# Issuing TensorE, VectorE and ScalarE in program order through the woven stretches of a four-layer network

## The chip, the cores and the metric

The kernel runs on one core of one Trainium2 chip, in fp32 throughout. The metric is the device time of one execution in microseconds (us), as the median of several runs; lower is better. One further execution is recorded by the hardware profiler. Its span, from the first instruction to the last, is given beside its own time.

## The reference

The input `x` is 8 images of 56 x 56 positions with 192 channels. Each of four layers adds something to it. Each layer first normalises it with a group norm `_gn` over 32 groups (a sample's groups of 6 channels over all positions).

```python
# layers 0 and 1
p, q, v = silu(x @ p_w.T + p_b), silu(x @ q_w.T + q_b), silu(x @ v_w.T + v_b)   # 192 -> 576
qv = q * v
o1 = _toeplitz(qv along w, a1)     # a1, a2: from a small MLP of the distance, times a decay
o2 = _toeplitz(qv along h, a2)     # one 56-tap kernel to each side, per channel
x = x + (p * (o1 + o2)) @ o_w.T + o_b          # with x normalised by _gn on the right
# layer 2
y = conv 7x7, depthwise (_gn(x)); y = layernorm(y); x = x + gamma * (gelu(y @ w0 + b0) @ w1 + b1)
# layer 3: attention in shifted 7x7 windows, 6 heads of 32, with position bias and masks
x = x + softmax(q @ k.T * s + bias) @ v @ Wfc + bfc
```

## The kernel before, in words

**Storage.** The 8 samples lie as 4 pairs. A pair's 2 x 192 channels fill three blocks of 128 partitions (128, 128, and 64 + 64). Two pairs are worked on at a time, named by `j0` = 0 or 2. So `Q(1, 2)` is the q and v projection of layer 1 for pairs 2 and 3. Intermediate results (`qv`, `L_sum`, `x1`, `x2`, `yd`) go through DRAM.

**Generators.** Each job is a Python generator that emits a piece of work and then yields the time that its author reckons for it.

- `tno_qv` (L207, called Q): for each of 25 groups of tokens, tile x is normalised on ScalarE (L228). Then come units of 512 output columns (a last one of 128): matmuls on TensorE (L245) into one or two PSUM tiles, a VectorE add of the bias (L254), and, in `multiply`, a Silu on ScalarE (L264), q times v on VectorE (L267) and the store through SP (L270). `multiply` of a unit is emitted at the head of the next unit, ahead of that unit's matmuls.
- `tno_toeplitz` (L317 to L376, called TZ): 18 rounds, an `along` and a `turned` kind in turn for nine blocks of 64 channels and two directions. `along` is TensorE matmuls of a qv tile `q` with Toeplitz matrices `tm` (L343) and a ScalarE copy (L350), in 8 groups. `turned` is 8 groups of TensorE transposes (L360) and a VectorE copy or add (L363, L366). After the eighth group of `along` ScalarE issues the loads for two rounds on: the half L317 (SP issues the other half) or the whole of L320, and two DMAs of L331. Each yield stands for four groups, 3.2 us.
- `tno_out` (called O): 28 steps of 224 tokens. A step has p's projection of this tile and the output projection of the one before, interleaved on TensorE (L460 to L499), Silus on ScalarE (L504, L521), the gate p * (o1 + o2) on VectorE (L531, L532), the residual sums (L514, L517), a POOL store (L115), and the normalisation of the next tile on VectorE (L442), which comes last.
- `conv` (loads L692 and L696): `turn` normalises a tile on ScalarE (L710), transposes it on TensorE (L722), and copies it on VectorE (L733) and ScalarE (L731); there are 7 tiles with two channel blocks (part 0) and 7 with one (part 1). `group` does 7 x 7 taps as 16 matmuls (L742) and a ScalarE copy (L749).
- `mlp`: layer norm (L832 to L844), transposes and scaling (L864, L866), expansion and gelu (L881, L890), and contraction (L961 to L979).
- `attention`: projections (L1102, L1112, L1155), scores (L1185), turned probabilities (L1223 to L1233), weighted sums (L1245), and `out` in two halves (L1271, with VectorE's L1282). The table `order` says at each of four places of a group whether a step of the next unit's projection (0) or of the last unit's `out` (1) is emitted.

**Order of the work.** `weave` runs a lane: it emits a step of the lane's generator, then as many steps of a second generator as its share of the time asks for. Near the end of a job it starts the next one (`begin`), so that its first loads are emitted early; a step that yields None adds no time. The lanes are, in order: Q(0,0); Q(0,2) with TZ(0,0); O(0,0) then Q(1,0) with TZ(0,2); O(0,2) then Q(1,2) with TZ(1,0); O(1,0) with TZ(1,2); O(1,2) with the first convolution; the MLP with the second convolution; the rest of the MLP with the head of the attention; and the attention.

What an engine executes, and in which order, isn't the order of emission: the framework's scheduler chooses for every engine from what has been emitted, by its own estimates. `manual_schedule(engines=...)` switches this off for the named engines within a block; these then get their instructions in the order of the program. The PSUM pool has 4 tiles of two banks (`bank2`); the SBUF pool `tp` has 3 buffers a name (`t6`, `t8`, `t4`), `q` has 2 and `cv`'s x tile 2.

Of the kernel before, what the change touches and what calls it, by code (L numbers as in the profile page):

```python
# [15 lines left out]
AX = mybir.AxisListType  # L16
PSUM = bass.MemoryType.PSUM
DRAM = bass.MemoryType.DRAM

B, H, W, C = 8, 56, 56, 192  # L20
T = H * W
# [10 lines left out]
def view(ap, offset, dims):  # L32

    return bass.AP(ap.tensor, ap.offset + offset, [ap.ap[0], *dims])


class Net:
# [371 lines left out]
        for f in late:  # L409
            store(*f)  # L410

    def tno_out(self, L, j0, xs, gn, o, ys, gn_next):

# [1 line left out]
        N = 224  # L417
# [10 lines left out]
        def load_x(j, t):  # L428

            x = p.tile([128, 3, 2 * N], F32, name="t6")  # L430
            self.load_pair(x, xs, j, slice(t * N, (t + 2) * N))
            return x

        def load_s(j, t):
            s = p.tile([128, 9, N], F32, name="t8")
            nc.sync.dma_start(s, o[j, :, :, t * N : (t + 1) * N].rearrange("k p t -> p k t"))
            return s

        def normalize(j, x):
            xn = p.tile([128, 3, N], F32, name="t4")  # L440
            for k in range(3):
                nc.vector.tensor_scalar(  # L442
                    xn[:, k, :], x[:, k, :], gn[:, j, k, 0:1], gn[:, j, k, 1:2], ALU.mult, ALU.add
                )
            return xn
# [96 lines left out]
        before = None  # L542
        x2 = load_x(*tiles[0])
        s = load_s(*tiles[0])
        yield 0.0
        xn = normalize(j0, x2[:, :, :N])
        done = None
        for n, (j, t) in enumerate(tiles):
            self.norm_part()
# [6 lines left out]
            x = x2[:, :, t % 2 * N : t % 2 * N + N]  # L556
            now = (j, t, x, s, st, xn)
            after = None
            if n + 1 < len(tiles):
# [3 lines left out]
                if t % 2:  # L563
                    x2 = x2_next
                at = (t + 1) % 2 * N
                after = tiles[n + 1][0], x2[:, :, at : at + N]
            xn = step(now, before, after)
# [47 lines left out]
    def tno_layers(self, x0, x1, x2, gn, last):  # L615


        tc, nc = self.tc, self.nc
        LS = ("L0", "L1")
        tables = [  # L620
            [self.dram.tile([D1, 112], F32, name=f"{L}_tab{d}") for d in range(2)] for L in LS
        ]
        qvs = {

            j0: self.dram.tile([D1 // 32, 64 * W, 128], F32, name=f"qv{j0}") for j0 in (0, 2)
        }
        o = [self.dram.tile([B // 2, 9, 128, T], F32, name=f"{L}_sum") for L in LS]
        x = (x0, x1, x2)
        with ExitStack() as ctx, ExitStack() as wqp:
            self.wqp = wqp.enter_context(tc.tile_pool(name="wqp", bufs=1, side="right"))  # L630
            self.tp = ctx.enter_context(tc.tile_pool(name="tp", bufs=3))
            Q = lambda i, j0: self.tno_qv(LS[i], j0, x[i], gn[i], qvs[j0])
            O = lambda i, j0: self.tno_out(LS[i], j0, x[i], gn[i], o[i], x[i + 1], gn[i + 1])
            TZ = lambda i, j0: self.tno_toeplitz(j0, tables[i], qvs[j0], o[i])
            QT, OT, TZT = 25 * 2.25 * 5.3, 28 * 10.7, 8 + 72 * 3.2

            with tc.tile_pool(name="tab", bufs=2) as tab:
                self.input_stats(x0, gn[0], 0, tab)
                self.decay_tables("L0", tab, tables[0])
                first = Q(0, 0)  # L640
                for n in range(20):
                    next(first)
                self.input_stats(x0, gn[0], 2, tab)
                none = tab.tile([112, 512], F32, name="none", bufs=1)
                nc.gpsimd.memset(none, 0.0)
                for qv in qvs.values():
                    to = qv[:, T:].rearrange("n (p k) e -> p n (k e)", p=112)
                    nc.gpsimd.dma_start(to, view(none, 0, [[0, D1 // 32], [1, 512]]))
                self.decay_tables("L1", tab, tables[1])
                lanes = [[(first, QT)], [(Q(0, 2), QT)], [(O(0, 0), OT), (Q(1, 0), QT)]]  # L650
                lanes += [[(O(0, 2), OT), (Q(1, 2), QT)], [(O(1, 0), OT)], [(O(1, 2), OT)]]
                self.weave(lanes[0], after=lanes[1][0][0])
            with tc.tile_pool(name="tz", bufs=1) as self.tz:
                self.tms = []
                for i in range(2):
                    tm = self.tz.tile([120, 32 * H + 8], F32, name=f"tm{i}")
                    nc.gpsimd.memset(tm, 0.0)
                    self.tms.append(tm)
                for n, tz in enumerate((TZ(0, 0), TZ(0, 2), TZ(1, 0), TZ(1, 2))):
                    self.weave(lanes[n + 1], tz, lanes[n + 2][0][0], TZT)  # L660
                    if n == 2:
                        wqp.close()
            self.weave(lanes[5], **last())

# [317 lines left out]
    def attention(self, L, xs, gn3, gnd, ys, vd):  # L984
# [6 lines left out]
        nc, tc, inp = self.nc, self.tc, self.inp  # L991
# [7 lines left out]
        if True:  # L999
# [72 lines left out]
            def normalize(b, ra, rb):  # L1072

                ja, sa = b % 4, b // 4
                gb = gr[ja // 2][:, ja % 2 + 2 * sa]
                for c, n, c2 in ((3, 53, 0), (0, 3, 53)):
                    nc.vector.tensor_scalar(
                        view(xa, c2, [[W, 28], [1, n]]),
                        view(ra, c, [[W, 28], [1, n]]),
                        gn3[:, ja, sa, 0:1],  # L1080
                        gn3[:, ja, sa, 1:2],
                        ALU.mult,
                        ALU.add,
                    )
                    nc.scalar.activation(
                        view(xb, c2, [[W, 16], [1, n]]),
                        view(rb, c, [[W, 16], [1, n]]),
                        AF.Identity,
                        bias=gb[:, 1:2],
                        scale=gb[:, 0:1],  # L1090
                    )
# [229 lines left out]
            late = None  # L1321


            order = ((0, 0, 0, 0), (0, 1, 1, 0), (0, 0, 0, 0))
            for n in range(len(units) + 1):
                if n < len(units):
                    (b, hh), (v, qf, kf) = units[n], now
# [234 lines left out]
```

## Time and profile before

| | us |
|---|---|
| median of 3 runs | 6437.01 (6429.92 to 6446.78) |
| the profiled execution's own time | 6428.51 |
| its span | 6426.7 |
| mean granted TensorE clock | 0.943 |

The span by stretches, each cut at the place where a lane changes, to about 10 us:

| stretch, us | work | length | TensorE busy | clock |
|---|---|---|---|---|
| 0 to 480 | statistics, tables, Q(0,0) | 480 | 393.5 | 0.97 |
| 480 to 1090 | Q(0,2) + TZ(0,0) | 610 | 535.0 | 0.93 |
| 1090 to 1625 | O(0,0) + TZ(0,2) | 535 | 470.5 | 0.93 |
| 1625 to 2085 | Q(1,0) + TZ(0,2) | 460 | 427.0 | 0.98 |
| 2085 to 2660 | O(0,2) + TZ(1,0) | 575 | 509.1 | 0.91 |
| 2660 to 3130 | Q(1,2) + TZ(1,0) | 470 | 437.0 | 0.97 |
| 3130 to 3830 | O(1,0) + TZ(1,2) | 700 | 598.5 | 0.90 |
| 3830 to 4340 | O(1,2) + convolution | 510 | 478.6 | 0.95 |
| 4340 to 4960 | MLP + convolution | 620 | 591.1 | 0.98 |
| 4960 to 5450 | MLP | 490 | 489.9 | 1.00 |
| 5450 to 6427 | attention | 977 | 853.5 | 0.91 |

TensorE's clock is granted by a throttle; 1.00 is full speed, and 0.93 means that some of the stretch ran at less. A busy TensorE at a lower clock takes longer for the same work, so busy time alone doesn't show it. In the profile, PE is TensorE, DVE VectorE, ACT ScalarE, POOL GpSimd and SP SyncE; a trailing q (ACTq) is the engine's instruction sequencer, which issues its DMAs. "PE bank L360 <- ACT ot L350" reads: TensorE, about to run line 360 for tile `bank`, waited for ScalarE's line 350, which writes `ot`.

### The profile page before, as it was taken

The numbers are of one execution on the slowest core, as the hardware profiler recorded it, in microseconds if no ns is written. First come the engines' busy times: TensorE is split into PE (matmuls) and PEld (weight loads), VectorE is DVE, ScalarE is ACT, GpSimd is POOL, SyncE is SP. The second block draws the span as 40 slices with busy tenths as digits, with TensorE's granted clock in tenths as the row PEclk, the third lists the DMA queues.
The fourth block names the chain that finished last, engine by engine and source line by source line (L and its number), as shares of the span: only waits on it lengthen the run. The fifth ranks groups of instructions, "written<-read, shape, count | busy, mean of one in ns | idle before, by whom it ended". The sixth has DMA issues, their size and how long they took to land.

```text
span 6426.7 us, 151998 instructions
## 1 busy us (share of the span) xinstructions
PE 5783.7 (90%) x68832; PEld 4566.2 (71%) x68832; DVE 2860.1 (45%) x4858; ACT 2148.7 (33%) x2736; POOL 635.6 (10%) x829
## 2 busy tenths in 40 slices
PE   5998898899999899898888889998999999898897
PEld 3777787787777778777777778885666444666665
DVE  6554555344555444455434343324212322555555
ACT  2444343232444222344232323224323333333332
POOL 0000000000000000000000010000000100333332
PEclk9998999999999999999988999999999999999998
DMA  7448887777675677675698865664444322443432
GB/s 247 116 145 217 225 253 182 209 201 214 182 200 163 178 214 204 186 213 161 174 228 213 256 198 193 218 237 127 166 152 152 93 61 59 73 87 85 90 82 56
DMA packets 1240518, 1078.47 MB, mean 168 GB/s; under 512 B 452704, under 2 KB 1186912, under 8 KB 1224448
## 3 DMA queue, kind: packets, MB, share of 16 engines
q1 hardware_dynamic: 825768, 620.03, 34.9%
q10 hardware_dynamic: 378648, 247.74, 15.1%
q0 software_dynamic: 35456, 200.98, 9.8%
q8 instruction: 541, 8.86, 0.6%
q14 instruction: 105, 0.86, 0.0%
HBM read 712.50 MB, written 356.12 MB: 166 GB/s over the span
## 4 chain that ended last, share of the span: by engine, by line
PE 70%; DVE 10%; DMA 8%; ACT 5%; issue 3%; ACTq 2%; POOL 1%; SPq 1%; DVEq 0%; POOLq 0%
PE bank L245 16%; PE bank L360 7%; PE bank L881 6%; PE bank L460 5%; PE bank L470 5%; PE bank L343 5%; PE bank L742 5%; PE bank L961 4%; PE bank L1155 2%; PE bank L975 2%; DMA qv<-t 2%; PE bank L475 2%; PE bank L492 2%; ACT ot L350 2%; DVE t L254 2%
## 5 line engine op out<-in xcount | busy, mean ns | idle before, releaser
L245 PE MATMUL bank<-wq,t 64*128 64x256 f32 (+5 forms) x8000 | 1319.9, 372 | 66.9 <-ACT ot L350 49.1
L245 PEld LDWEIGHTS bank<-wq,t 64*128 64x128 f32 (+3 forms) x8000 | 1041.0, 189 | 319.1 <-issue 104.9
L264 ACT ACTIVATE t<-t 128x2048 f32<-128x2048 f32 (+1 forms) x300 | 439.9, 1482 | 960.8 <-DVE t L254 872.4
L254 DVE TENSOR_TENSOR t<-bank,wq 128x1024 f32<-128x1024 f32 (+2 forms) x500 | 540.2, 1113 | 477.1 <-PE bank L245 476.2
L360 PE MATMUL bank<-ident,ot 120*128 120x120 f32 x4032 | 549.0, 300 | 162.7 <-ACT ot L350 64.7
L360 PEld LDWEIGHTS bank<-ident,ot 120*128 120x128 f32 x4032 | 494.6, 160 | 222.7 <-DVE s L363 78.1
L504 ACT ACTIVATE t<-bank,wo 128x448 f32<-128x448 f32 x448 | 247.5, 635 | 1065.3 <-PE bank L475 795.8
L343 PE MATMUL bank<-q,tm 56*64 56x112 f32 x18432 | 522.6, 266 | 70.8 <-issue 32.8
L531 DVE TENSOR_TENSOR t<-t,t 128x896 f32<-128x896 f32 x224 | 241.4, 1090 | 752.9 <-ACT t L504 752.0
L343 PEld LDWEIGHTS bank<-q,tm 56*64 56x64 f32 x18432 | 482.1, 138 | 105.9 <-issue 57.1
L350 ACT COPY ot<-bank 128x896 f32<-128x896 f32 x576 | 481.6, 916 | 158.2 <-PE bank L343 157.4
L460 PE MATMUL bank<-t,wo 128*128 128x224 f32 x1792 | 405.1, 382 | 85.8 <-ACT t L504 46.4
L460 PEld LDWEIGHTS bank<-t,wo 128*128 128x128 f32 x1792 | 358.0, 207 | 106.5 <-ACT t L504 58.2
L267 DVE TENSOR_TENSOR t<-t 128x1024 f32<-128x1024 f32 (+1 forms) x300 | 280.5, 955 | 317.0 <-ACT t L264 253.8
L881 PE MATMUL bank<-z,w 128*128 128x448 f32 (+1 forms) x1344 | 413.2, 555 | 2.0 <-ACT h L890 2.0
L470 PE MATMUL bank<-t,wo 128*128 128x224 f32 x1792 | 367.2, 359 | 7.8 <-DVE t L531 4.9
L470 PEld LDWEIGHTS bank<-t,wo 128*128 128x128 f32 x1792 | 346.1, 194 | 11.9 <-DVE t L531 5.3
L363 DVE COPY s<-bank 128x784 f32<-128x784 f32 x288 | 267.7, 970 | 152.7 <-PE bank L360 122.9
L742 PEld LDWEIGHTS bank<-xt,cm 113*112 113x112 f32 x3072 | 309.2, 178 | 36.1 <-issue 31.7
L881 PEld LDWEIGHTS bank<-z,w 128*128 128x128 f32 (+1 forms) x1344 | 182.2, 189 | 205.5 <-issue 196.8
L376 POOL DMA_DIRECT2D L_sum<-s x288 | 141.0, 496 | 1821.5 <-DVE s L366 1816.0
L742 PE MATMUL bank<-xt,cm 113*112 113x108 f32 (+2 forms) x3072 | 317.4, 263 | 3.5 <-ACT h L890 2.4
(141 smaller groups left out, 6814.8 us busy)
## 6 DMA issues: line engine op xcount, KB each, us to landing
q<-qv ACTq DMA_DIRECT2D x36, 3584.0 KB
L_sum<-s POOLq DMA_DIRECT2D x288, 392.0 KB, 7.2
t<-L_sum SPq DMA_DIRECT2D x112, 1008.0 KB
qv<-t SPq DMA_DIRECT2D x192, 512.0 KB
cm<-in_L_cm SPq DMA_DIRECT2D x96, 896.0 KB
tm<-L_tab ACTq DMA_DIRECT2D x144, 392.0 KB
q<-qv SPq DMA_DIRECT2D x36, 1568.0 KB
q<-qv ACTq DMA_DIRECT2D x36, 1568.0 KB
```

Source lines behind the costliest of these rows:

```text
L245: nc.tensor.matmul(pp[:m, b, 256 * j : 256 * j + k], x[rows, j, 2 if part else b, s : s + m], w[rows, part, c0 + c : c0 + c + k],  start=p ...
L254: nc.vector.tensor_add(z[:m, c : c + k, :], view(pp[:m], 0, [[1, k], [256, 4]]), view(bias[:m], c0 + c, [[1, k], [0, 4]]),)
L264: nc.scalar.activation(z[:m, :n, :], z[:m, :n, :], AF.Silu)
L267: nc.vector.tensor_mul(prod[:m, :k], half[:, :, 0], half[:, :, 1])
L343: nc.tensor.matmul(pt[64 * s : 64 * s + 64, r, j * 112 : (j + 1) * 112], tm[rows, c * H : c * H + 64], q[rows, PR * s : PR * s + PR, 4 * c ...
L350: nc.scalar.copy(view(ot, 4 * g, [[112 * 32, 2], [32, 112], [1, 4]]), view(pt, 0, [[512, 2], [1, 112], [112, 4]]),)
L360: nc.tensor.transpose(pz[:, i, :120], ot[:120, at : at + 128], self.ident[:120, :120])
L363: nc.vector.tensor_copy(to, view(pz, 0, [[128, n], [64, 2], [1, 56]]))
L460: mm(gs[c // 2][:, b, c % 2 * 256 : c % 2 * 256 + N], pw[:, 0, 128 * c : 128 * c + 128], xn[:, b], start=c % 2 == 0, stop=False,)
L470: mm(P[:, b, :N], ow[:, c, 0:128], g[:, 4 * b + c], start=c == 0, stop=False)
L742: nc.tensor.matmul(pc[:, 128 * e + 4 * m0 : 128 * e + 4 * m1], cm[:113, e, k, :], xt[:, m0 - 1 + k : m1 - 1 + k, c + e, :], start=n == 0 a ...
L881: nc.tensor.matmul(phs[c][:, s, :TT], w0[rows, part, at : at + 128], z[rows, Z[2 if part else s], :], start=part == flip, stop=part != flip,)
```

## The change

The four weaves with TZ, the weave of O(1,2) with the first convolution, and the weave of the MLP with the second run under `manual_schedule` for TensorE, ScalarE and VectorE. POOL and SP stay with the scheduler, as do Q(0,0), the last part of the MLP, and the attention. `tno_out` gets a flag `early`: set for all but O(1,2), it makes the job yield None after its first loads, and normalise its first tile before its yield of 0.0 instead of after it, so one step of the previous lane earlier. In the attention's second group, a step of the projection stands between the two halves of `out`.

```diff
+ENGINES = {mybir.EngineType.PE, mybir.EngineType.Activation, mybir.EngineType.DVE}

-    def tno_out(self, L, j0, xs, gn, o, ys, gn_next):
+    def tno_out(self, L, j0, xs, gn, o, ys, gn_next, early):
...
         x2 = load_x(*tiles[0])
         s = load_s(*tiles[0])
+        if early:
+            yield None
+            xn = normalize(j0, x2[:, :, :N])
         yield 0.0
-        xn = normalize(j0, x2[:, :, :N])
+        if not early:
+            xn = normalize(j0, x2[:, :, :N])
...
-            O = lambda i, j0: self.tno_out(LS[i], j0, x[i], gn[i], o[i], x[i + 1], gn[i + 1])
+            O = lambda i, j0, early=True: self.tno_out(LS[i], j0, x[i], gn[i], o[i], x[i + 1], gn[i + 1], early)
...
-                lanes += [[(O(0, 2), OT), (Q(1, 2), QT)], [(O(1, 0), OT)], [(O(1, 2), OT)]]
+                lanes += [[(O(0, 2), OT), (Q(1, 2), QT)], [(O(1, 0), OT)], [(O(1, 2, False), OT)]]
                 self.weave(lanes[0], after=lanes[1][0][0])
-            with tc.tile_pool(name="tz", bufs=1) as self.tz:
+            in_order = tc.manual_schedule(engines=ENGINES)
+            with tc.tile_pool(name="tz", bufs=1) as self.tz, in_order:
...
-            self.weave(lanes[5], **last())
+            rest = last()
+            with tc.manual_schedule(engines=ENGINES):
+                self.weave(lanes[5], **rest)
...
-            order = ((0, 0, 0, 0), (0, 1, 1, 0), (0, 0, 0, 0))
+            order = ((0, 0, 0, 0), (0, 1, 0, 1), (0, 0, 0, 0))
...
-                net.weave([(net.part(mlp, first), first)], convs[1], None, net.CONV_TIME, 0.02, 0.97)
+                with tc.manual_schedule(engines=ENGINES):
+                    net.weave(
+                        [(net.part(mlp, first), first)], convs[1], None, net.CONV_TIME, 0.02, 0.97
+                    )
```

## The prediction

> **What bounds the kernel now.** I read the busy shares first.
>
> ```profile
> PE 5783.7 (90%) x68832; PEld 4566.2 (71%) x68832; DVE 2860.1 (45%) x4858; ACT 2148.7 (33%) x2736; POOL 635.6 (10%) x829
> ```
>
> TensorE sets the pace; the others have room on average, so they matter only where TensorE waits for one of them. Next the stretches of the program, cut where the traces of its tiles change. Columns: stretch, length, busy time of each engine (instructions), granted TensorE clock, DMA share, GB/s.
>
> ```profile
> 480.00:1090.00 610.00, 534.97 (x7282) 466.66 (x7283) 307.57 (x320) 244.03 (x275) 34.80 (x72) 0.93 0.83 219
> ...
> 3830.00:4340.00 510.00, 478.64 (x3754) 428.36 (x3752) 154.91 (x320) 138.48 (x240) 37.30 (x41) 0.95 0.63 221
> 4340.00:4960.00 620.00, 591.05 (x3342) 381.08 (x3342) 160.70 (x528) 206.53 (x277) 37.82 (x71) 0.98 0.45 147
> ```
>
> These are Q(0,2) with Toeplitz products, O(1,2) with the first convolution, and the MLP with the second. In the first, TensorE idles 75 us, and a clock of 0.93 costs about 610 x 0.07 = 43 us more. The later Q stretches, 1625 to 2085 and 2660 to 3130, have a clock of 0.98 and 0.97 and a DMA share of 0.66 and 0.67. Then who is waited for, by stretch (us in total, times, longest): four rows of the first, then one each of O(1,2) with the convolution and of the attention (5450 to the end).
>
> ```profile
> PE bank L360 <- ACT ot L350: 33.2, 9, 6.3
> PE bank L343 <- ACT ot L350: 11.7, 7, 4.8
> PE bank L343 <- issue: 10.5, 5, 2.8
> PE bank L343 <- DVE t L254: 8.6, 2, 8.1
> ...
> PE bank L722 <- ACT x L710: 19.1, 6, 5.3
> ...
> PE bank L1271 <- DVE ra L1282: 47.0, 30, 3.6
> ```
>
> In Q stretches TensorE waits for ScalarE's copies L350, since Silus (1.9 us) and normalisations (0.6 us) stand ahead of them; L245 waits 4.5 more for them. The convolution's normalisations L710 cost 19.1, and 4.0 more in the MLP. Last, one load event in the timeline (start, duration): ScalarE alone,
>
> ```profile
> 841.08 1.63 ACTq L317 DMA_DIRECT2D q<-qv  x1
> 842.81 13.86 ACTq L331 DMA_DIRECT2D tm<-L_tab  x1
> 856.77 2.43 ACT L264 ACTIVATE t<-t 128x512 f32<-128x512 f32 x2 [14.81 <-DVE s L363]
> ```
>
> and TensorE and VectorE meanwhile.
>
> ```profile
> 848.01 6.13 PE L360 MATMUL bank<-ident,ot 120*128 120x120 f32 x56
> 849.53 7.13 DVE L363 COPY s<-bank 128x784 f32<-128x784 f32 x8
> ...
> 861.18 1.55 DVE L267 TENSOR_TENSOR t<-t 128x256 f32<-128x256 f32 x2
> ```
>
> ScalarE is held 13.86 us by issuing one load behind another. TensorE doesn't notice, because VectorE goes on with adds and L363 copies and takes the multiply L267 last.
>
> **What the skill says.** "TensorE: Matmul & The Clock Gate", Part 1: the clock halves after an idle window of about 3.4 us and returns after a busy one. The trace agrees:
>
> ```profile
> 1144.20 3.35 PE L460 MATMUL bank<-t,wo 128*128 128x224 f32 x8 [17.48 <-ACT t L504]
> ```
>
> 8 matmuls take 3.35 us here; at 1119.62, 5 take 2.06 and elsewhere 16 take 3.29. I price each gap over 3.4 us at 1.7 us of lost work (half a window). "PSUM — Partial Sum Buffer", Engine vs sequencer instructions: ScalarE's and VectorE's queues are strict first-in-first-out. So a waiting multiply holds all behind it. The event above shows the same for ScalarE. "DMA: Bandwidth & Descriptors", Issuing engines are not separate DMA queues: transfers interleave on the same 16 engines whoever issues; the 0.83 DMA share in the first stretch fits, so moving an issue doesn't make a load quicker.
>
> **The change part by part.** I laid the built kernels' instruction orders side by side. TensorE's order hardly changes, POOL's not at all; on SP the last qv stores of a lane fall behind an x and a weight load. ScalarE's and VectorE's change much. So the question is only how late they are. The sum is made on the profiled execution (6428.5 us, span 6426.7); the median 6437.0 lies 8.5 higher, and I add the sum to the median.
>
> A. Copies first in Q lanes. The four L350 (0.914 us) now come before Silu and normalisations. Of 33.2 + 11.7 + 4.5 = 49.4 us in the first stretch I remove 28: TensorE makes a group each 0.83 us, so the last copy is late anyhow. In the two later Q stretches L245 waits for L350 23.6 and 21.1 us; I remove 40 of the sum. Of the 43 us of clock I give back 20. A = -88; bounds -137 (all waits and clock) and -30 (the same waits come back as waits on adds).
>
> B. Loads hold Silu and multiply. In the new order the Silu of unit n-1 stands after the last copy and the loads L317, L331, L331; VectorE takes multiply n-1 (L267), add n (L254), then L363. Let D be the long L331, T0 the end of the last L343. ACT is free at T0 + D + 2.0 (as above: 856.7 against 840.8), Silu 1.9, multiply 1.2, add 1.2: banks of unit n come free at T0 + D + 6.3. TensorE can go on with unit n (5.6) and two of four L360 groups (1.6), until T0 + 7.2: a stall of D - 0.9; with the next unit in between it is near D - 4.9, and with the short unit's case between. I take D - 2.7. In the first stretch the eight D are 6.84, 12.37, 12.89, 10.00, 6.83, 13.86, 8.30, 6.95, mean 9.76: 8 x 7.1 = 57. In the two later Q stretches three each near 7.0: 6 x 4.3 = 26. Eight gaps cross 3.4 us, some twice: 16 of clock. B = +99. Queued behind the waiting multiply: add n, the L363 copies, then TensorE for banks. Bounds: 0 (loads earlier in the step drain faster) and +170 (every D 13.9).
>
> C. Starts of lanes 2 to 4. Today ScalarE and SP issue q and matrix loads before O begins; the gate tile of O waits on a store queued behind them, L460 waits 17.5, 13.5 and 14.1 us for L504, and 5.4, 5.3, 5.4 for L442. After, loads are issued after two or three O steps and `early` puts L442 into the lane before: 61 us go. But the first L343 waits for 8.5 MB (two q tiles 3.2 + 3.7, matrices 1.6; at about 240 GB/s 35 us, O steps cover three times 9): I put back 38, and take 10 of clock. C = -33; bounds -75 and +20.
>
> D. L442 behind L514 and L517 on VectorE. Where O follows O with no Toeplitz or convolution piece between (about 20 places, by the order: starts of lanes, lane 4, lane 5), TensorE waits for 0.68 + 0.45 + 0.44 + 0.2 hop = 1.8 us. D = +36; bounds +5, +45. With a piece of 3.3 us between, it is hidden.
>
> E. Convolution's tokens. L710 is today issued as soon as x lands. After, it stands behind the previous step's L521, L731, L890 (1.0 us each), L966 (1.1) or L979 (0.7), and TensorE's L722 comes right after. A tile of part 0: 1.0 + 4 x 0.745 - 0.8 (three transposes of 0.27 overlap) makes 3.2; behind a second gelu 4.2. I take 3.7, seven tiles: 26. Part 1: 1.1 + 2 x 0.745 - 0.3 = 2.3, seven: 16. Two convolutions: 84, less the 23 paid now: +61. Half the 14 larger gaps cost clock: 12. E = +73. Bounds +10 (steps come where ScalarE is idle) and +110.
>
> F. Attention. A project step goes between the halves of `out`. Thirty waits on L1282 are 15 pairs, a long and a short one, 47 us; the long one probably moves to L1155, for the bank. F = -10; bounds -45, +5.
>
> Costed at nothing: TensorE's order, as its own work is 5783.7 us either way; and the qv stores moved behind two loads on SP, which only the next lane's q loads await: the O steps in C cover them, and without these they would cost some 11 us a lane (0.8 + 1.8 MB at 240 GB/s).
>
> Sum: -88 + 99 - 33 + 36 + 73 - 10 = +77. Forecast 6437 + 77 = **6514** (6505 on the profiled execution).
>
> **Rivals.**
> 1. Not slower: copies first wins. The mechanism is in the Q lanes: 49 + 43 in the first, 45 in the others, if no regular gap is left to halve the clock; C -50; B with D at the 6.9 already seen three times, 14 x 4.2 = 59. Sum -92 - 45 + 59 - 50 + 36 + 73 - 10 = -29: **6408**. B decides: without it the sum is -88, so it breaks even at D = 2.7 + 88/14 = 9.0. For it: ScalarE is only 40% busy (244 of 610), so order, not work, makes these waits. Against: D's mean is 9.8 there now. If E is half hidden too and L1282's waits vanish, 6335.
> 2. Slower still: every load takes 13.9 us, since qv stores and q loads collide (DMA share 0.83): B 157 for 83, and each new gap halves the clock (24 more): 6437 + 175 = **6612**. Against: the later Q stretches show D 7 at share 0.66.
> 3. Nothing: the order doesn't matter as TensorE's is the same, and waits only change names: **6437**. Against: in the event above TensorE runs past a held Silu only since VectorE has the multiply last, and that place is lost.
>
> **How the numbers follow.** Forecast 0.40, rival 1 0.33, rival 2 0.18, rival 3 0.09. 0.3% (19 us) is about what a measurement here can tell from no change. Faster 0.31: most of rival 1. Same 0.12: rival 3 and some of rival 1. Slower 0.57. The forecast's own range is 6465 to 6565; to hold 8 in 10 the range takes most of rivals 1 and 2: 6365 to 6610.
>
> **What would show it.** A: rows L360, L343, L245 <- ACT L350 shrink to under half. B: rows of L360 or L245 waiting for DVE L254 of 2 to 11 us, each beside a long L331; if absent, B is wrong. C: L460 <- L504 waits over 10 us gone, L343 <- DMA q or tm at the lane's start. D: about 20 waits L460 <- L442 of 1.8. E: L722 <- L710 rises from 23 to about 84 us. F: L1271 <- L1282 shrinks, L1155 grows. Wrong altogether if the clock of the first stretch rises to 0.98, or long L331 issues shrink below 3 us.

## The result and the profile after

The changed kernel takes 6877.7 us (median; 6871.4 to 6878.1), the kernel before 6435.6 in the same comparison: a ratio of 1.0682 (1.0664 to 1.0701). It is 442 us slower. The forecast had the direction right and the size wrong: it said +77. The kernel before took between 6416 and 6436 us (medians) in the six comparisons of this document, so a difference between runs of different comparisons is uncertain by some 20 us.

In the changed kernel the lines of the projections and Toeplitz products have numbers higher by 2 (L360 is now L362, L254 is L256), those of the convolution, the MLP and the attention by 9 (L710 is L719, L1155 is L1164).

The busy shares come first, as before:

```profile
PE 5808.7 (84%) x68832; PEld 4584.8 (67%) x68832; DVE 2868.6 (42%) x4858; ACT 2146.5 (31%) x2736; POOL 636.7 (9%) x829
```

All engines are busy for about as long as before (TensorE 25 us longer, at a mean clock of 0.919 for 0.943). So nearly all of the loss is TensorE standing still: its idle time went from 6426.7 - 5783.7 = 643 to 6875.9 - 5808.7 = 1067 us. By stretch, cut at the first and last matmul of a job (stretch, length, busy time by engine, clock, DMA share, GB/s):

```profile
480.00:1291.00 811.00, 575.88 (x7470) 493.72 (x7472) 317.00 (x334) 256.72 (x286) 34.81 (x72) 0.85 0.66 173
1813.00:2395.00 582.00, 483.44 (x4938) 398.76 (x4937) 273.93 (x299) 210.32 (x232) 20.87 (x42) 0.90 0.55 150
...
4201.00:4808.00 607.00, 534.52 (x3996) 469.95 (x3995) 187.63 (x415) 144.70 (x253) 39.91 (x44) 0.92 0.58 197
4808.00:5440.00 632.00, 577.42 (x3152) 365.22 (x3152) 147.44 (x457) 203.06 (x266) 35.48 (x68) 0.95 0.43 138
```

The first is Q(0,2), the second Q(1,0), then O(1,2) with the convolution, and the MLP with the second one. Cut at the same events, before and after:

| job | before | after | change |
|---|---|---|---|
| up to the first Toeplitz matmul | 477 | 486 | +9 |
| Q(0,2) | 638 | 806 | +167 |
| O(0,0) | 507 | 521 | +14 |
| Q(1,0) | 500 | 582 | +82 |
| O(0,2) | 514 | 523 | +10 |
| Q(1,2) | 507 | 576 | +69 |
| O(1,0) | 684 | 707 | +23 |
| O(1,2), convolution | 556 | 607 | +51 |
| all after it | 2044 | 2068 | +24 |

The three Q stretches lost 318 of 449 us of span. Whom TensorE waits for, over the whole span (us, times, longest):

```profile
PE bank L362 <- DVE t L256: 237.8, 32, 14.2
PE bank L247 <- ACT t L230: 139.9, 31, 17.7
PE bank L362 <- ACT t L506: 116.1, 19, 11.7
PE bank L731 <- ACT x L719: 60.8, 78, 2.9
PE bank L345 <- DMA tm<-L_tab: 46.0, 7, 17.9
...
PE bank L1164 <- DVE ra L1291: 42.2, 14, 3.6
...
PE bank L462 <- DVE t L444: 41.3, 13, 8.9
PE bank L362 <- ACT ot L352: 39.7, 25, 2.0
```

The first row is the forecast's step B at nearly three times its size; the second is in no step of the forecast; the third was costed nowhere. The last row shows that step A happened: the longest wait of a transpose for a copy is now 2.0 us, and was 6.3. Now one load event of the first stretch, ScalarE alone:

```profile
593.20 0.34 ACTq L319 DMA_DIRECT2D q<-qv  x1
593.29 0.94 ACT L352 COPY ot<-bank 128x896 f32<-128x896 f32 x1
593.64 16.43 ACTq L333 DMA_DIRECT2D tm<-L_tab  x2
610.17 1.91 ACT L266 ACTIVATE t<-t 128x2048 f32<-128x2048 f32 x1 [15.95 <-issue]
```

then VectorE:

```profile
612.11 1.22 DVE L269 TENSOR_TENSOR t<-t 128x1024 f32<-128x1024 f32 x1 [26.72 <-ACT t L266]
613.26 2.35 DVE L256 TENSOR_TENSOR t<-bank,wq 128x1024 f32<-128x1024 f32 x2
615.52 0.96 DVE L365 COPY s<-bank 128x784 f32<-128x784 f32 x1
```

and TensorE:

```profile
598.67 1.65 PE L362 MATMUL bank<-ident,ot 120*128 120x120 f32 x14
614.53 1.86 PE L362 MATMUL bank<-ident,ot 120*128 120x120 f32 x8 [14.21 <-DVE t L256]
```

This is the chain that the forecast described, link by link. Two matrix issues hold ScalarE for 16.4 us: it starts nothing else until they are done. The Silu L266 stands behind them, the multiply L269 behind the Silu, the add L256 behind the multiply; TensorE has done the two groups for which banks were free, and waits 14.2 us for the next.

Summed over the trace, ScalarE's DMA issues take 599 us before and 1,122 after. Nearly all of it is now in the matrix loads:

```profile
L333 ACTq DMA_DIRECT2D tm<-L_tab x144: 313/8542/16855, 470.0 to 4112.0; - x144
```

(shortest, median, longest in ns). That is 144 issues in 72 rounds, and 1,081 us in all, 15 a round. Before, they took 396 us.

### The profile page after: what moved, and what is told of

Read it like the earlier page. It is cut to its first block, busy times and chain, and to the rows that moved or that the text cites. A ratio compares the mean times of both kernels' runs of the same rounds, so it can differ in the third digit from the quotient of the medians.

```text
span 6875.9 us, 152088 instructions
## 1 busy us (share of the span) xinstructions
PE 5808.7 (84%) x68832; PEld 4584.8 (67%) x68832; DVE 2868.6 (42%) x4858; ACT 2146.5 (31%) x2736; POOL 636.7 (9%) x829
## 5 line engine op out<-in xcount | busy, mean ns | idle before, releaser
L247 PE MATMUL bank<-wq,t 64*128 64x256 f32 (+5 forms) x8000 | 1361.8, 377 | 153.8 <-ACT t L230 139.9
L247 PEld LDWEIGHTS bank<-wq,t 64*128 64x128 f32 (+3 forms) x8000 | 1065.8, 193 | 426.2 <-ACT t L230 156.1
L362 PE MATMUL bank<-ident,ot 120*128 120x120 f32 x4032 | 548.9, 302 | 404.8 <-DVE t L256 237.8
L362 PEld LDWEIGHTS bank<-ident,ot 120*128 120x128 f32 x4032 | 502.8, 162 | 456.0 <-DVE t L256 246.2
L266 ACT ACTIVATE t<-t 128x2048 f32<-128x2048 f32 (+1 forms) x300 | 443.1, 1485 | 1116.8 <-DVE t L256 708.7
L269 DVE TENSOR_TENSOR t<-t 128x1024 f32<-128x1024 f32 (+1 forms) x300 | 284.5, 955 | 897.4 <-ACT t L266 888.7
L256 DVE TENSOR_TENSOR t<-bank,wq 128x1024 f32<-128x1024 f32 (+2 forms) x500 | 538.6, 1111 | 238.1 <-PE bank L247 237.9
L506 ACT ACTIVATE t<-bank,wo 128x448 f32<-128x448 f32 x448 | 247.5, 634 | 1194.1 <-PE bank L477 718.4
L345 PE MATMUL bank<-q,tm 56*64 56x112 f32 x18432 | 512.8, 264 | 113.8 <-DMA tm<-L_tab 46.0
L345 PEld LDWEIGHTS bank<-q,tm 56*64 56x64 f32 x18432 | 475.7, 137 | 142.2 <-issue 105.1
L516 DVE SCALAR_TENSOR_TENSOR t<-bank,wo,t 128x448 f32<-128x448 f32 x112 | 76.6, 684 | 1071.9 <-PE bank L501 1071.9
L462 PE MATMUL bank<-t,wo 128*128 128x224 f32 x1792 | 389.2, 373 | 47.3 <-DVE t L444 41.3
L472 PE MATMUL bank<-t,wo 128*128 128x224 f32 x1792 | 371.6, 362 | 43.7 <-DVE t L533 21.6
L462 PEld LDWEIGHTS bank<-t,wo 128*128 128x128 f32 x1792 | 350.7, 202 | 63.7 <-issue 47.6
L472 PEld LDWEIGHTS bank<-t,wo 128*128 128x128 f32 x1792 | 348.3, 196 | 51.8 <-issue 40.5
```

Source lines behind the costliest of these rows:

```text
L247: nc.tensor.matmul(pp[:m, b, 256 * j : 256 * j + k], x[rows, j, 2 if part else b, s : s + m], w[rows, part, c0 + c : c0 + c + k],  start=p ...
L256: nc.vector.tensor_add(z[:m, c : c + k, :], view(pp[:m], 0, [[1, k], [256, 4]]), view(bias[:m], c0 + c, [[1, k], [0, 4]]),)
L266: nc.scalar.activation(z[:m, :n, :], z[:m, :n, :], AF.Silu)
L269: nc.vector.tensor_mul(prod[:m, :k], half[:, :, 0], half[:, :, 1])
L345: nc.tensor.matmul(pt[64 * s : 64 * s + 64, r, j * 112 : (j + 1) * 112], tm[rows, c * H : c * H + 64], q[rows, PR * s : PR * s + PR, 4 * c ...
L362: nc.tensor.transpose(pz[:, i, :120], ot[:120, at : at + 128], self.ident[:120, :120])
```

## The experiments

Theory 1 says that the loads' issue in ScalarE's program order holds Silu, multiply and adds, and so TensorE. Theory 2 says that the fixed compute order on VectorE or ScalarE does it, whoever issues the loads. Each run's ratio is to the kernel before, with its 95% interval.

**All Toeplitz loads on SP.**

```diff
-                for half, eng in ((0, nc.sync), (1, nc.scalar)):
+                for half, eng in ((0, nc.sync), (1, nc.sync)):
...
-                nc.scalar.dma_start(q.rearrange("p i e -> p (i e)"), of)
+                nc.sync.dma_start(q.rearrange("p i e -> p (i e)"), of)
...
-                nc.scalar.dma_start(to.rearrange("p (c w) -> p c w", w=H), src)
+                nc.sync.dma_start(to.rearrange("p (c w) -> p c w", w=H), src)
```

> The changed kernel, but SP issues all of the Toeplitz loads (the half of q, the whole q, and the matrices) that ScalarE issues in it. Theory 1 (the loads' issue holds ScalarE, its Silu, the multiply behind it on VectorE, and so TensorE's banks): the waits of the transposes for the bias add (238 us), of transposes and Toeplitz matmuls for the gate's Silu (116 + 16) and part of those for the matrices go: about -350 us, near 6,530. Theory 2 (the fixed order multiply, add, copies on VectorE costs this by itself, whoever issues the loads): 6,820 to 6,880. Between them, 6,600 to 6,750, if SP now blocks and delays x loads and qv stores.

Measured 6349.4 us, ratio 0.9887 (0.9867 to 0.9908): 528 us less than the changed kernel, and faster than the kernel before by 1.1%. This is theory 1, and more than its own estimate. L362 <- L256 fell from 238 to 21 us, L362 <- L506 left the upper rows, and L247 <- L230 fell from 140 to 51: so some 88 us of the waits for the normalisation came from the held ScalarE as well.

**Normalisation two units earlier.**

```diff
-                    if c0 == 1024 and s + 128 >= n and g + 1 < groups:
+                    if c0 == 0 and s + 128 >= n and g + 1 < groups:
```

> The changed kernel, but Q's six normalisations of the next x tile are emitted two units earlier (at the first instead of the last unit of the second half tile). Theory 1 (they stand right before the unit that needs them, behind a Silu): the waits of the unit for them, 140 us, fall under 30 us: about 6,760. Theory 2 (the load of x is late, or the hold by the Toeplitz loads causes these waits too): within 30 us of 6,878.

Measured 6794.0 us, ratio 1.0581 (1.0562 to 1.0599): 84 less, not 118. The waits for L230 fell from 140 to 24 us, and L362 <- L256 rose from 238 to 290: with ScalarE still held, part of the wait moved one step down.

**Program order in the Toeplitz weaves only, and in the convolutions' only.** The edits leave out `manual_schedule` in the other place and set the attention's order back.

> Program order only in the four weaves with Toeplitz products, with the early normalisation of O; both convolutions and the attention's order as in the kernel before. Theory 1 (the Toeplitz lanes hold most of the loss): 6,800, by taking the changes of the stretches with a convolution, +51 and about +30, off 6,878. Theory 2 (the convolution's stretches matter as much as forecast, 73 us, or more through the following stretch): 6,780 or less.

> Program order only in the two weaves with a convolution; Toeplitz weaves left to the scheduler, with the early normalisation of O, and the attention's order as before. Forecast's step for the convolution: +73, so 6,510; from the stretches of the changed kernel: +51 and +30, 6,515. A rival: the stretches lose time only since the Toeplitz part before hands them its waits: 6,450.

Toeplitz only: 6792.6 us, ratio 1.0578 (1.0559 to 1.0598). Convolutions only: 6541.9 us, ratio 1.0179 (1.0152 to 1.0206), 119 more than the 6422.7 of before. The Toeplitz lanes hold most of the loss, and the convolutions cost more than the 73 forecast. In the second run the stretch of O(1,2) grew by 58 us and what follows by 46; the changed kernel, which also has the new attention order, grew by only 24 there.

**The loads on SP in the kernel before.**

> The kernel before, the scheduler at work everywhere, with all Toeplitz loads issued by SP. Theory 1 (program order itself pays in the Toeplitz lanes once ScalarE is free of the loads): the scheduler gains less from it than program order did; 6,390 to 6,440, as its waits for a held ScalarE are only those of O for the gate's Silu, 46 us. Theory 2 (only who issues matters; the order adds nothing or costs): 6,250 to 6,350, as the run of program order with the loads on SP (6,349) or below it, since the convolution's loss isn't in it.

Measured 6319.2 us, ratio 0.9830 (0.9797 to 0.9862). This is theory 2's number: most of the gain is from who issues. But by stretch the order counts: with all loads on SP the three Q stretches take 679, 525 and 518 us under the scheduler and 631, 510 and 507 in program order, 74 us less. O's stretches take 441, 438 and 643 under the scheduler and 450, 452 and 647 in program order, 27 us more. So program order is worth some 47 us in the Toeplitz lanes when the loads are equal (with O's early normalisation, which the run under the scheduler lacks), and then loses about 70 in the convolutions and what follows.

**Loads still on ScalarE, but apart.** Each matrix is emitted after one half of the turned groups instead of right behind the q load (`matrices` gets the halves to load as an argument).

```diff
...
                         loaded.append(load(n + 2))
-                        matrices(n + 2)
                     yield 3.2
...
                 turned(d, ot, s, u // 4, u % 4 * 7, 7)
+                if u % 4 == 3 and n + 2 < NS:
+                    matrices(n + 2, (u // 4,))
                 if u % 4 == 3:
```

> The changed kernel, all loads still on ScalarE, but the two matrix loads are emitted apart: after the first and the second half of the turned groups, instead of right behind the q load. If the issue is held because load stands right behind load (each waits for the one before to drain), the time in ScalarE's matrix issues falls from 1,081 to under 400 us and the kernel to 6,550 or less. If ScalarE is held as long by any such load wherever it stands, 6,800 or more.

Measured 6408.2 us, ratio 0.9970 (0.9960 to 0.9980): 470 us less than the changed kernel with no load taken off ScalarE. The matrix issues fell to 635 us, not under 400: one was still held 9.6 us (at 625.43), 7.5 us after its q load. Rounds in which both matrices were held over 3 us fell from 36 to 18, and a Silu now stands between the q load and the last matrix (L266 at 618.82 in this round), so that the multiply and the adds behind it go on. L362 <- L256 fell from 238 to 19 us, and L362 <- L506 left the upper rows. So it is the place of the issues that counts, not only their sum.

**Matrices ahead of q.** The two emissions are swapped.

> The changed kernel with one swap: in each round ScalarE issues the two matrix loads ahead of the q load instead of behind it, all three still back to back. If an issue is held until what its own queue has ahead of it has drained (a q load is 1.6 or 3.6 MB, the matrices 0.4 MB each), a q load behind two small ones is held far shorter than two small ones behind a q load: ScalarE's issues sum to under 500 us instead of 1,122 and the kernel comes to 6,500 or less. If three issues in a row are what holds, in whichever order, the sum stays near 1,100 and the time near 6,878.

Measured 6612.0 us, ratio 1.0298 (1.0265 to 1.0330), issues 698 us. This lies between the two readings: three issues in a row aren't held alike in every order, but turning them round doesn't free ScalarE either. The matrices still take 347 us, 294 of it the second of each pair, and q behind them 351, where in the changed kernel ScalarE's q issues, ahead of the matrices, took 41.

**One engine back to the scheduler.**

> The changed kernel, but program order only for TensorE and VectorE; the scheduler orders ScalarE, with its loads and Silus. Theory 1 (loads standing ahead of the Silu in ScalarE's order are the loss): below 6,500. Theory 2 (VectorE's fixed order, multiply before add, is enough to lose it): over 6,700.

> The changed kernel, but program order only for TensorE and ScalarE; the scheduler orders VectorE. ScalarE is held as long (1,100 us of issues). If the chain needs VectorE's fixed order (a multiply that waits for the held Silu with the adds behind it), the 238 us of waits for the bias add mostly go: 6,600. If ScalarE's hold reaches TensorE anyhow, by the scheduler choosing the same order or by the gate's Silu and the normalisation, 6,800 or more.

ScalarE scheduled: 6560.3 us, ratio 1.0224 (1.0209 to 1.0240). VectorE scheduled: 6746.5 us, ratio 1.0515 (1.0499 to 1.0531). So ScalarE's order is worth 317 us and VectorE's 131. Without VectorE's order the rows for the bias add do go, but the held ScalarE reaches TensorE by its normalisation instead: L247 <- L230 rises to 211.7 us. Neither run meets its number; theory 1 is nearer in both, and VectorE's order is a link of the chain, not its cause. With ScalarE scheduled the kernel is still 144 us slower than before: ScalarE's issues are down to 623 us, but L362 <- L256 still waits 89 us and L462 <- L444 101.

**Which loads, and which queue.**

> The changed kernel, but SP issues all q loads; the matrix loads stay on ScalarE at their places. Own-queue theory (an issue is held by what its own engine has issued before it): ScalarE's matrix issues, with 0.8 MB a round as all that is on that queue, fall from 1,081 to under 150 us, and the kernel to about 6,400. Shared-engine theory (any issue is held while the 16 DMA engines have a q load to move, whichever queue it is on): they stay over 700 us and the kernel over 6,600.

> The changed kernel, but SP issues the matrix loads; q loads stay on ScalarE. Own-queue theory: a q load on ScalarE has only the last round's q load ahead of it, some 30 us earlier, so its 72 issues are held under 150 us in all, and the kernel comes near 6,350 to 6,400. Shared-engine theory: over 500 us, and over 6,550.

With q on SP: 6577.3 us, ratio 1.0236 (1.0206 to 1.0266). ScalarE's matrix issues still take 621 us. ScalarE at one load event, with nothing but matrices on its queue:

```profile
616.16 0.34 ACTq L333 DMA_DIRECT2D tm<-L_tab  x1
616.25 0.94 ACT L352 COPY ot<-bank 128x896 f32<-128x896 f32 x1
616.60 15.36 ACTq L333 DMA_DIRECT2D tm<-L_tab  x1
632.07 1.91 ACT L266 ACTIVATE t<-t 128x2048 f32<-128x2048 f32 x1 [14.88 <-issue]
```

SP had issued the q load at 616.15. With the matrices on SP: 6301.9 us, ratio 0.9807 (0.9783 to 0.9831), and ScalarE's q issues take 53 us in all; ScalarE there:

```profile
593.73 0.35 ACTq L322 DMA_DIRECT2D q<-qv  x1
593.74 0.93 ACT L352 COPY ot<-bank 128x896 f32<-128x896 f32 x1
594.53 1.95 ACT L266 ACTIVATE t<-t 128x2048 f32<-128x2048 f32 x1
```

Each theory fails in one run, and the pairs in the traces say why. With q on SP, the first matrix issue of a pair took 0.34 us in the median and the second 7.62: the second is held behind the first, which stands alone ahead of it in ScalarE's queue. How long goes with the load on the other queue: from 513 to 1068 us the second was held 3.2 to 4.2 us beside half q loads and 8.6 to 15.4 beside whole ones. And q loads aren't spared as such: with nothing ahead of them they took 53 us, behind the matrices 351.

What makes the difference is the number of pieces ahead, not their bytes. A load moves in pieces, which the trace lists: a half q load is 3,136 pieces of 512 bytes (1.6 MB), a whole one 128 of 28,672 (3.7 MB), a matrix 1,792 of 224 (0.4 MB). In the changed kernel the first matrix behind a half q load was held in all 36 rounds (6.1 us or more, median 8.9), behind a whole one in none (median 0.42), though that is more than twice the bytes; the second matrix was held in all 72. Counting what was still to move in ScalarE's own queue when an issue began: at least 1,920 pieces ahead of each of the 112 issues that took over 2.5 us, and at most 1,580 ahead of each of the 96 that took under 0.7. No run varies the number of pieces of one load to test this. For this kernel it is enough that the matrix loads must not stand in ScalarE's order. That the hold lasts as long as the traffic shows in the DMA view of the changed kernel over the event above, from 593 to 611 us, in 40 slices:

```profile
DMA  1004999999999999999999999999999999999955
```

The share is at 90% or more from 594.8 us on and falls in the last two slices, from 610.1 us, when ScalarE goes on. Why an issue has to wait at such a number of pieces isn't settled.

**The attention's order alone**, in the kernel before.

> The kernel before with only the attention's order changed. The forecast's step for it was -10 (-45 to +5); the stretch after the first convolution's lane was 35 us shorter where the order was new and the convolutions were left to the scheduler. So -35 (6,400) if that is the swap's; within 15 us of before if it came from elsewhere.

Measured 6392.2 us, ratio 0.9962 (0.9948 to 0.9977), 24 less than the 6416.2 beside it. The long wait moved from L1271 to L1155 (43.5 us, 14 times, against 47.0, 30 times), as forecast. But the waits lost only 3.5 us. The clock in the attention rose from 0.91 to 0.94, and TensorE was busy 821.8 us there for 853.5.

**Towards a better version.** First the convolution's normalisation (`normal`, the loop of L719 taken out of `tokens`) a tile earlier, with the loads on SP and Q's normalisation two units earlier; then, with the last two and without the first, program order in the Toeplitz weaves alone.

```diff
...
+                if t == 0:
+                    normal(*tiles[done], xq[0])
                 if done + 1 < len(tiles):
                     xq.append(load(*tiles[done + 1]))
                 part = tiles[done][0]
                 tokens(*tiles[done], xq.pop(0))
+                if t + 1 < NT:
+                    normal(*tiles[done + 1], xq[0])
```

> The changed kernel with three edits: Toeplitz loads on SP, Q's normalisation two units earlier, and a convolution tile's normalisation emitted right after the tile before it instead of with its own transposes. If the waits of the transposes for it (61 us) are what program order costs in the convolution: 6,349 - 51 - 50 = 6,250. If they come back as waits of the Silus and gelus behind it: 6,300.

> What the runs so far ask for: program order in the Toeplitz weaves alone, their loads on SP, Q's normalisation two units earlier, the attention's new order; the convolutions' weaves left to the scheduler. If the effects add: 6,349 - 51 (waits for the normalisation) - 95 (the convolution's stretches) = 6,205. If the convolution's stretches start later or the early normalisation only moves a wait to the bias add: 6,250 to 6,300.

All three: 6275.7 us, ratio 0.9772 (0.9738 to 0.9806), halfway between its two numbers; the waits of the convolution's transposes for the normalisation fell from 61 to 40 only. Toeplitz weaves alone: 6199.9 us, ratio 0.9655 (0.9621 to 0.9688); here the effects add.

> The best so far (program order in the Toeplitz weaves alone, loads on SP, Q's normalisation two units earlier, the attention's new order: 6,200), with O's first normalisation at its old place. The early normalisation was to save the waits of O's first matmuls for it at three starts of lanes, 5.4 us each: 6,215. If those waits are for the x load and not for the order, within 8 us of 6,200.

> As the best so far, but only the q loads on SP and the matrices on ScalarE. Own-queue theory: SP, relieved of 144 issues, holds the stores and x loads less; 6,170 to 6,200. If ScalarE is held again by the matrices: 6,250 or more.

> Program order in the Toeplitz weaves alone, only the matrix loads on SP, Q's normalisation two units earlier, O's at its old place, the attention's new order. From the run with the matrices alone moved (6,302): less about 95 for the convolutions left to the scheduler and 30 to 40 for the waits for the normalisation: 6,165 to 6,180. If the stages don't add up, 6,195 as with all loads on SP.

Without O's early normalisation the time is 6194.5 us, ratio 0.9645 (0.9619 to 0.9672): no difference. With q on SP and matrices on ScalarE it is 6392.8, ratio 0.9947 (0.9924 to 0.9971): ScalarE is held again (609 us). With the matrices alone on SP and no early normalisation of O it is **6147.7 us, ratio 0.9565 (0.9532 to 0.9599)**: faster than both kernels. The largest waits of its first Q stretch:

```profile
PE bank L345 <- issue: 29.4, 8, 6.6
PE bank L462 <- DVE t L444: 8.6, 1, 8.6
PE bank L362 <- ACT ot L352: 8.0, 7, 1.2
```

No wait of the transposes for the adds or for the gate's Silu is left among them. How much of these 280 us is due to program order isn't shown: no run has the matrices alone on SP under the scheduler. Where both orders were run with equal loads, program order was worth the 47 us above.

## Why the prediction was wrong

**A, copies first (-88): right in kind.** Waits for the copies in the Q stretches went from 94 us (49.4 + 23.6 + 21.1) to 17, where 68 were to go. With equal loads the order is worth 74 us in these stretches. But none of it is seen in the sum, as ScalarE was now held by loads.

**B, loads hold Silu and multiply (+99): the step that failed.** The chain was right; its size was not, and three terms of the sum were wrong. First, the hold D was taken from the kernel before, 9.76 us in the first stretch and 7.0 later, where one matrix load stood ahead of the q load and one behind it. In the new order both stand behind it, and the pair was held 16.4 us in the event shown and 13.7 in the mean of the Q stretches. Second, only the 14 half q loads were counted; it is every round, 30 in the Q stretches, as the pair behind a whole q load is held too. The trace of before had one such round, at 671.64, and the forecast's list of eight D leaves it out:

```profile
671.64 0.35 ACTq L320 DMA_DIRECT2D q<-qv  x1
672.03 0.42 ACTq L331 DMA_DIRECT2D tm<-L_tab  x1
672.55 12.35 ACTq L331 DMA_DIRECT2D tm<-L_tab  x1
```

The same in the changed kernel:

```profile
640.43 0.35 ACTq L322 DMA_DIRECT2D q<-qv  x1
640.82 16.64 ACTq L333 DMA_DIRECT2D tm<-L_tab  x2
```

Third, O was left out: its gate Silu L506 is behind the same issues, with 116 us of waits of the transposes and 16 of the Toeplitz matmuls. The trace of before has this case as well: an L331 of 15.28 us at 1296.88, with L504 right behind it. Measured, the waits for L256 and L506 together are 370 us, where 83 were forecast. The forecast's citation of the Trainium skill, "DMA: Bandwidth & Descriptors", Issuing engines are not separate DMA queues, goes with this: the page adds that the time to initiate a DMA is usually small relative to the DMA itself. Here a matrix issue took 8.5 us in the median, while its 392 KB would move in about 2.6 us at the trace's mean of 157 GB/s (an estimate). The measurement decides.

**A step that was missing.** Q's six normalisations of the next tile, which the scheduler had issued well ahead, came to stand behind a Silu and right before their unit: 140 us of L247 <- L230, of which 51 stay without any hold of ScalarE. The forecast saw this order and priced only what the normalisations no longer delay.

**C, starts of lanes (-33): not met.** The waits of 17.5, 13.5 and 14.1 us for L504 went, but L345 now waits 46 us for matrices, some 34 of it at these starts, and L462 <- L444 is 8.7, 8.3 and 8.9 at the lanes' starts, longer than the 5.4 that `early` was to remove. The tile of the normalisation waits there for a qv store ("DMA qv<-t" before L444), so issuing it earlier gains nothing; the run without `early` agrees (6194.5 for 6199.9). The 38 us that the forecast put back doesn't follow from its own figures: 35 less 27 is 8 a lane. O's stretches grew by 47 us together; the largest new row in them is the one for L506.

**D, normalisation behind the residual sums (+36): the price right, the count wrong.** The single wait is about 1.6 us, but outside the starts of lanes there are ten of them, not twenty, and the whole row is 41 us for 33 before.

**E, convolution (+73): about +104** in the two stretches of the run with program order there alone. The waits for L719 came to 61 us in the changed kernel for the 84 forecast. The clock fell from 0.95 to 0.92 and from 0.98 to 0.95 in the two stretches, and other rows grew that the forecast doesn't name: L873 <- L875 22.9 us for 10.8, L472 <- L533 21.6 for 4.9.

**F, attention (-10): the right direction, by another way.** 24 us were measured, of which the waits are 3.5; the rest goes with the higher clock. Why the clock rose isn't shown.

Rival 2 named the right excess, long holds, and stopped at 6,612, since it too multiplied 14 events. Rival 1 asked for short holds (D under 9.0). The run with the matrices on SP has none of them on ScalarE, and is faster than the kernel before, though by the move of the loads as well as by the order.

## What to carry to other kernels

When an engine is set to program order, look first at the DMAs that it issues. A scheduler that puts compute ahead of an issue hides the time of the issue; in program order every compute instruction behind it is held, with all who wait for that. Don't carry the duration of an issue over from the old profile: here it depended on how many pieces stood ahead of it in its queue, and so on the order of the loads. And list each instruction whose neighbours changed, not only those whose wait you expect to lose: the normalisation here was seen and not priced.

## What the runs showed of the hardware that was not expected

Whether ScalarE was held by issuing a load went with the number of pieces still ahead in its own queue, not with their bytes: in the changed kernel no issue with at most 1,580 pieces ahead took over 2.5 us, and none with 1,920 or more took under 0.7. A 392 KB load in 224-byte pieces held it for up to 16.9 us there, and for up to 17.3 us when the q loads were on SP. The same q loads cost ScalarE 53 us for 72 issues with the matrices on SP, and 351 us behind the matrices. In the profile the 1,081 us of the matrix issues aren't counted in ScalarE's busy share, which was 31% after and 33% before.
